# Real and imaginary halves of a scan swapped by ScalarE copies within PSUM instead of by a matmul

## The chip, the cores and the metric

One core of a Trainium2 chip runs the whole program. The metric is the device time of one execution in microseconds (us), as the median of several executions.

## The reference

A four-layer residual network on eight images of 64 channels and 128 x 128 points, all in float32. Layer 0 is a deformable convolution, layer 1 a 3 x 3 convolution, layer 2 a bidirectional state-space scan along rows and along columns, layer 3 a nearest-neighbour layer. The change is in layer 2, whose core is

```python
def _s5_scan(u, lam_re, lam_im, B_re, B_im, C_re, C_im, D, log_step):
    lam = lam_re + 1j * lam_im
    ...
    Bu = jnp.einsum('blh,ph->blp', u.astype(lam.dtype), B_bar)
    A = jnp.broadcast_to(lam_bar, Bu.shape)
    _, xf = jax.lax.associative_scan(_binop, (A, Bu), axis=1)
    _, xb = jax.lax.associative_scan(_binop, (A, Bu[:, ::-1]), axis=1)
    xs = jnp.concatenate([xf, xb[:, ::-1]], axis=-1)
    return 2.0 * jnp.real(jnp.einsum('blp,hp->blh', xs, Cc)) + D * u
```

with 64 complex states, on every image once with rows as the sequence and once with columns. Around it stand a layer norm before, a Gelu, a second layer norm and a product of small matrices after.

## The kernel before, in words

The eight images are handled as four pairs; a pair lies on 128 partitions (two images of 64 channels). First `deform` does layer 0 for all pairs: GpSimd (POOL) gathers, and VectorE (DVE) weights what was gathered. Then `rest` takes the four pairs one after the other, each through `conv3x3` (layer 1), `scan_layer` (layer 2) and, beside the next pair's work, `neighbours` (layer 3).

In the scan a complex state is kept as 128 partitions: its real part on the lower 64 and its imaginary part on the upper 64. A sequence is cut into groups of 4 x 256 points, 16 groups (`NG`) to a pair and direction. A complex rotation turns the recurrence into one with a real decay, which DVE's scan instruction can do; the rotation multiplies by a cosine, and adds the other half times a sine. For that second term the two halves must change places, one of them with its sign changed.

Three methods of `Scan` matter:

- `drive` makes the input of the recurrence: two matmuls into PSUM tile `pv`, a ScalarE (ACT) copy of it to SBUF tile `v` (L1256), a matmul of `v` with the constant 128 x 128 matrix `turn`, which swaps the halves and sets the sign, into PSUM tile `pt` (L1257), two DVE products of `pv` with cosines and of `pt` with sines (L1260), and their sum on POOL (L1261).
- `scan` runs the recurrence: a small matmul `pn` (L1269), an ACT copy of two columns (L1274), and two DVE scans into `z` (L1276).
- `rebuilt` turns a scan's result back: a matmul of it with `turn` into PSUM tile `zt` (L1301), a POOL product with cosines (L1305), a DVE product of `zt` with sines into `xt` (L1306), and their difference on POOL (L1307). For the backward scan the result comes back from device memory as `zb`.

`pv`, `pt` and `zt` share one PSUM pool tag, `b`, with two buffers; they take turns. `xt` and `v` have one buffer each.

Per pair these run in three stages, called A, B and C here:

- Stage A: `first_norm` (the layer norm, 8 steps) beside the backward scan along rows (`ways[0].back`). 16 drives.
- Stage B: `ways[0].ahead`, with `ways[1].back` beside it: per group one forward and one backward `drive`, two `rebuilt`, the output matmuls `py` (L1321), Gelu on ACT and a DVE sum `h` (L1323, L1324), the matmuls `pc` (L1339) with ACT's square and copy of them (L1340, L1342), the DVE chain `ln` of 15 small instructions that makes a reciprocal root (lines 112 to 122), a POOL product `ms` (L1353), transposes `tp` (L1357), and a DVE sum into the image, `room` (L1359).
- Stage C: `ways[1].ahead`, the same with one `drive` per group, plus DVE's `bn` statistics (L1362).

Each engine runs its own instructions strictly in the order that a scheduler writes down when the program is built. That order comes from the scheduler's own estimates, so a change to a few instructions can move all the others of the same stage. Where an instruction must wait for another engine, everything behind it on its own engine waits too.

Of the kernel before, what the change touches and what calls it, by code (L numbers as in the profile page):

```python
# [9 lines left out]
F32 = mybir.dt.float32  # L10
I32 = mybir.dt.int32
AF = mybir.ActivationFunctionType
ALU = mybir.AluOpType
# [3 lines left out]
P = 128  # L17
# [9 lines left out]
NS = 64  # L27
T = 4
NB = 256
# [13 lines left out]
class Net:  # L43
# [596 lines left out]
    def setup_scan(self, pp, ptag):  # L640
# [10 lines left out]
        tc, nc, ins, keep = self.tc, self.nc, self.ins, self.keep  # L651
        self.dirs = []
        with tc.tile_pool(name="b_scan_setup", bufs=1) as sp:
# [45 lines left out]
            sign = sp.tile([P, 1], F32, name="sign")  # L699
# [7 lines left out]
            swap = sp.tile([P, P], F32, name="swap")  # L707
            nc.vector.tensor_scalar(swap, col, swap_p, None, ALU.is_equal)

            self.turn = keep.tile([P, P], F32, name="turn")  # L710
            nc.vector.tensor_scalar(self.turn, swap, sign, -1.0, ALU.mult, ALU.mult)
            eye = self.ident

            qre, qim = (sp.tile([P, T + 1, 2], F32, name=f"q{n}") for n in ("re", "im"))
# [26 lines left out]
            for d in range(2):  # L741
# [8 lines left out]
                cs, sn = tabs[:, COS + 1 : COS + 1 + NB], tabs[:, SIN + 1 : SIN + 1 + NB]  # L750
# [15 lines left out]
                t2 = sp.tile([P, P], F32, tag="t2", name=f"t2_{d}")  # L766
                nc.vector.tensor_scalar(t2, swap, ssin[:, one], None, ALU.mult)
                nc.vector.scalar_tensor_tensor(tabs[:, ROT : ROT + P], eye, cs[:, NB - 1 : NB], t2, ALU.mult, ALU.add)

                u_, v_ = (sp.tile([P, 2, C], F32, tag=f"b{k}", name=f"b{k}_{d}") for k in "uv")  # L770
                for i in range(2):
# [444 lines left out]
class Scan:  # L1216
# [31 lines left out]
    def drive(self, f, g, fx):  # L1248

        nc, net, wp, tabs, tag = self.nc, self.net, self.wp, self.tabs, f"{self.p}_{self.d}{f}_{g}"  # L1250
        pv, pt = (net.ps.tile([P, 2, NB], F32, tag="b", name=f"{n}{tag}") for n in ("pv", "pt"))
        for h in range(2):
            at = MAT + (2 * f + h) * P
            nc.tensor.matmul(pv, lhsT=tabs[:, at : at + P], rhs=fx[:, :, h, :], start=h == 0, stop=h == 1)  # L1254
        v = wp.tile([P, 2, NB], F32, tag="v", name=f"v{tag}", bufs=1)
        nc.scalar.copy(v, pv)  # L1256
        nc.tensor.matmul(pt, lhsT=net.turn, rhs=v, start=True, stop=True)  # L1257
        u = wp.tile([P, 2, NB], F32, tag="u", name=f"u{tag}")
        for o, src, at in ((u, pv, COS), (v, pt, SIN)):
            nc.vector.tensor_mul(o, src[:, :, ::-1] if f else src, self.both(at + 1))  # L1260
        nc.gpsimd.tensor_add(u, u, v)  # L1261
        return u

    def scan(self, f, g, u, last, ztag):

        nc, wp, tabs, tag = self.nc, self.wp, self.tabs, f"{self.p}_{self.d}{f}_{g}"
        if last is not None:
            pn = self.net.ps1.tile([P, 2], F32, tag="bs", name=f"pn{tag}")
            nc.tensor.matmul(pn, lhsT=tabs[:, ROT : ROT + P], rhs=last[:, :, NB], start=True, stop=True)  # L1269
        z = wp.tile([P, 2, NB + 1], F32, tag=ztag, name=f"z{tag}", bufs=1 if ztag == "zbk" else 2)  # L1270
        if last is None:
            nc.vector.memset(z[:, :, 0:1], 0.0)
        else:
            nc.scalar.copy(z[:, :, 0], pn)  # L1274
        for i in range(2):
            nc.vector.tensor_tensor_scan(z[:, i, 1 : NB + 1], tabs[:, DEC : DEC + 1].to_broadcast([P, NB]), u[:, i, :], z[:, i, 0:1], ALU.mult, ALU.add)  # L1276
        return z
# [16 lines left out]
    def rebuilt(self, f, g, zf):  # L1294

        nc, net, wp, tag = self.nc, self.net, self.wp, f"{self.p}_{self.d}_{g}"
        if f:
            zf = wp.tile([P, 2, NB], F32, tag="zb", name=f"zb{tag}", bufs=1)
            nc.sync.dma_start(zf, net.back[self.d][g])
        pt = net.ps.tile([P, 2, NB], F32, tag="b", name=f"zt{f}{tag}")  # L1300
        nc.tensor.matmul(pt, lhsT=net.turn, rhs=zf[:, :, 0:NB], start=True, stop=True)  # L1301
        x = wp.tile([P, 2, NB], F32, tag=f"x{f}", name=f"x{f}{tag}", bufs=1)
        t = wp.tile([P, 2, NB], F32, tag="xt", name=f"xt{f}{tag}", bufs=1)
        o = x[:, :, ::-1] if f else x
        nc.gpsimd.tensor_mul(o, zf[:, :, 0:NB], self.both(COS))  # L1305
        nc.vector.tensor_mul(t, pt, self.both(SIN))  # L1306
        nc.gpsimd.tensor_sub(o, o, t)  # L1307
        return f, x
# [133 lines left out]
```

## Time and profile before

| | |
|---|---|
| median of 10 runs | 16339.99 us (16328.91 to 16344.98) |
| the profiled execution: time | 16343.99 us |
| the profiled execution: span of the core | 16342.2 us, mean granted clock 0.824 |
| busy: PE (matmul) | 10862.0 us, 66% |
| busy: DVE | 11670.0 us, 71% |
| busy: ACT | 2880.8 us, 18% |
| busy: POOL | 10189.8 us, 62% |
| `deform` | from the start to about 11740 us |
| pair 0: stages A, B, C | about 11914 to 12111, to 12431, to 12689 us |

Busy shares are means over stages with different limits. `deform` takes the first 72% and holds nothing of the scans' loops. In the scans one group of stage B follows the other after 21.4 us, one group of stage C after 15.7 us, and one step of stage A after 20.5 us.

### The profile page before, as it was taken

To read this page: it belongs to the slowest core of one execution; us is meant where nothing else is said; L and a number is where in the kernel's file an instruction comes from. 1 tells how busy PE (TensorE), PEld (TensorE's weight loads), DVE (VectorE), ACT (ScalarE), POOL (GpSimd) and SP (SyncE) were. 2 spreads that over 40 slices of the span, in tenths; PEclk is the share of its full clock that TensorE was granted. 3 is DMA by queue.
4 is the path that set the end of the run, shared out by engine and by line. 5 is a ranking of instruction groups with operands and counts; after the bars stand their busy time and mean duration, and the time that the engine had idled before them with its cause. 6 is when DMAs were issued, how large, how long until landed. Compare 5 with 4: busy or idle time off the path is not lost. (4 is left out here: it accounts for less than half of the span.)

```text
span 16342.2 us, 119261 instructions
## 1 busy us (share of the span) xinstructions
PE 10862.0 (66%) x31736; PEld 3994.6 (24%) x31736; DVE 11670.0 (71%) x27948; ACT 2880.8 (18%) x4762; POOL 10189.8 (62%) x10484
## 2 busy tenths in 40 slices
PE   7864676367665535766556655643489788888896
PEld 2211122112211111211111111111135344344343
DVE  6777777777777777777777777777547558466566
ACT  1100111011000001100000000000144254243342
POOL 5777777777777777777777777777425135044142
PEclk9986797678887767988778877865699899999997
DMA  5434444344433334443333333333422533434223
GB/s 172 126 120 134 138 144 151 111 140 149 147 114 118 115 112 139 147 124 115 118 115 115 115 119 115 114 108 108 125 65 68 151 80 101 119 82 135 88 68 107
DMA packets 900135, 1933.41 MB, mean 118 GB/s; under 512 B 199932, under 2 KB 435844, under 8 KB 876420
## 3 DMA queue, kind: packets, MB, share of 16 engines
q0 software_dynamic: 442368, 1208.55, 25.0%
q1 hardware_dynamic: 382048, 679.50, 13.6%
q10 hardware_dynamic: 75044, 37.72, 1.1%
q8 instruction: 257, 4.21, 0.1%
q14 instruction: 418, 3.42, 0.1%
HBM read 1540.74 MB, written 208.10 MB: 107 GB/s over the span
## 5 line engine op out<-in xcount | busy, mean ns | idle before, releaser
L380 POOL DMA_INDIRECT g<-table,idx x9216 | 8717.0, 946 | 2823.2 <-issue 2633.8
L391 DVE TENSOR_TENSOR g<-g,corner_weights 128x256 f32<-128x256 f32 x9216 | 3777.6, 416 | 2707.8 <-DMA g<-table,idx 2670.4
L392 DVE TENSOR_REDUCE sm<-g 128x64 f32<-128x256 f32 x9216 | 5018.3, 580 | 8.8
L292 PE MATMUL po<-xe,wt 128*54 128x512 f32 (+3 forms) x8384 | 4299.3, 628 | 13.1 <-ACT ob L302 13.0
L398 PE MATMUL sp<-ident,sm 128*128 128x128 f32 x4096 | 1536.1, 380 | 4156.8 <-DVE sm L392 4142.5
L398 PEld LDWEIGHTS sp<-ident,sm 128*128 128x128 f32 x4096 | 629.3, 155 | 6725.4 <-DVE sm L392 5020.5
L403 ACT COPY s<-sp 128x512 f32<-128x512 f32 x1024 | 599.8, 586 | 8717.5 <-PE sp L398 8717.1
L292 PEld LDWEIGHTS po<-xe,wt 128*54 128x54 f32 x8384 | 902.4, 132 | 1344.5 <-issue 1061.9
L409 PE MATMUL yp<-s,wd 128*64 128x512 f32 (+1 forms) x2560 | 898.2, 711 | 25.7 <-ACT s L403 24.8
L891 POOL COPY l_yb<-ln_y 128x512 f32<-128x512 f32 x128 | 72.8, 612 | 1300.6 <-DVE ln_y L122 1300.6
L1261 POOL TENSOR_TENSOR u<-u,v 128x512 f32<-128x512 f32 x256 | 327.9, 1281 | 688.1 <-DVE v L1260 553.4
L607 PE MATMUL c<-room,l_w 128*64 128x508 f32 (+1 forms) x3072 | 740.8, 597 | 23.3 <-DMA room<-nx 13.4
L1353 POOL TENSOR_TENSOR ms<-ms,ln_y 128x512 f32<-128x512 f32 x256 | 274.0, 1090 | 641.4 <-DVE ln_y L122 619.3
L1243 ACT ACTIVATE fx<-room,ln_b,ln_g 128x512 f32<-128x512 f32 x512 | 639.2, 1292 | 170.8 <-DMA in<-fx 149.5
L1276 DVE TENSOR_TENSOR_SCAN z<-tabs,z,u 128x256 f32<-128x256 f32 x512 | 435.4, 876 | 214.5 <-POOL u L1261 185.9
L1254 PE MATMUL pv<-in,tabs 128*128 128x512 f32 x1024 | 509.4, 620 | 43.6 <-DVE u L1260 40.7
L1339 PE MATMUL pc<-outs,h 128*128 128x256 f32 x2048 | 498.1, 386 | 29.1 <-DVE h L1324 26.8
L1321 PE MATMUL py<-x,outs 128*128 128x512 f32 x1024 | 504.3, 596 | 7.9 <-POOL x L1307 7.4
L1321 PE MATMUL py<-in,outs 128*128 128x512 f32 x1024 | 506.8, 608 | 2.9 <-ACT h L1323 2.3
L1339 PEld LDWEIGHTS pc<-outs,h 128*128 128x128 f32 x2048 | 393.2, 193 | 205.9 <-issue 113.3
L1307 POOL TENSOR_TENSOR x<-x,xt 128x512 f32<-128x512 f32 x256 | 347.9, 1359 | 131.8 <-DVE xt L1306 131.5
L609 DVE TENSOR_TENSOR room<-room,c 128x512 f32<-128x512 f32 x128 | 88.1, 688 | 438.6 <-PE c L607 435.4
(416 smaller groups left out, 10184.2 us busy)
## 6 DMA issues: line engine op xcount, KB each, us to landing
g<-table,idx POOLq DMA_INDIRECT x9216, 2.7
in<-fx SPq DMA_DIRECT2D x1024, 128.0 KB
xe<-in_x_dram SPq DMA_DIRECT2D x56, 1408.0 KB
table<-q SPq DMA_DIRECT2D x256, 256.0 KB
y<-ys SPq DMA_DIRECT2D x128, 256.0 KB
room<-in_x_dram SPq DMA_DIRECT2D x64, 512.0 KB
yr<-y SPq DMA_DIRECT2D x64, 512.0 KB
room<-nx SPq DMA_DIRECT2D x256, 128.0 KB
```

Source lines behind the costliest of these rows:

```text
L292: nc.tensor.matmul(po[:, r0:r1, c0:c1], lhsT=wt[:, t, :], rhs=xe[:, row + r0 : row + r1, c0 + dx : c1 + dx], start=n == 0, stop=n == len(u ...
L380: nc.gpsimd.indirect_dma_start(out=tq[:, k, :], out_offset=None, in_=flat[i], in_offset=bass.IndirectOffsetOnAxis(ap=idx[:, at : at + 1], ...
L391: nc.vector.tensor_mul(t[:, ks], t[:, ks], w)
L392: nc.vector.tensor_reduce(sm[:, ks], t[:, ks].rearrange("p k q c -> p k c q"), axis=mybir.AxisListType.X, op=ALU.add)
L398: nc.tensor.transpose(sp[:, j, :], sm[:, j * P : (j + 1) * P], self.ident)
L403: nc.scalar.copy(st[i][:, :, m * P : (m + 1) * P], sp)
L409: nc.tensor.matmul(yp[half[i], :], lhsT=wd[rows, j, :], rhs=src[rows, :], start=j == 0, stop=j == 4)
L607: nc.tensor.matmul(o, lhsT=lt, rhs=mv, start=k < 2, stop=k >= len(calls) - 2)
L1243: nc.scalar.activation(fx[:, e].rearrange("p h (o m) -> p h o m", m=self.INNER), src[:, e::2], AF.Identity, bias=w["ln1_b"], scale=w["ln1_g"])
L1254: nc.tensor.matmul(pv, lhsT=tabs[:, at : at + P], rhs=fx[:, :, h, :], start=h == 0, stop=h == 1)
L1321: nc.tensor.matmul(py, lhsT=lt, rhs=mv, start=n == 0, stop=n == len(calls) - 1)
L1339: nc.tensor.matmul(pc[:, i], lhsT=hs[:, h, i, m * P : (m + 1) * P], rhs=self.outs[:, CEN : MIX + P], start=True, stop=True)
```

## The change

In `drive` and in `rebuilt` the matmul with `turn` is gone. A new method `swap` writes the two halves of the PSUM tile by two ACT copies of 64 partitions each, the upper half of the source to the lower half of the target and the other way round. In `drive` they read `pv` in PSUM, and the copy of `pv` to SBUF is gone too; in `rebuilt` they read the scan's result in SBUF. The sign that was in `turn` is multiplied into the table of sines once, when the tables are made; `turn` is no longer made.

```diff
@@ setup_scan
-            self.turn = keep.tile([P, P], F32, name="turn")
-            nc.vector.tensor_scalar(self.turn, swap, sign, -1.0, ALU.mult, ALU.mult)
...
+                nc.vector.tensor_scalar(sn, sn, sign, None, ALU.mult)
@@ drive
+        self.swap(pt, pv)
         v = wp.tile([P, 2, NB], F32, tag="v", name=f"v{tag}", bufs=1)
-        nc.scalar.copy(v, pv)
-        nc.tensor.matmul(pt, lhsT=net.turn, rhs=v, start=True, stop=True)
         u = wp.tile([P, 2, NB], F32, tag="u", name=f"u{tag}")
         for o, src, at in ((u, pv, COS), (v, pt, SIN)):
             nc.vector.tensor_mul(o, src[:, :, ::-1] if f else src, self.both(at + 1))
         nc.gpsimd.tensor_add(u, u, v)
         return u
+
+    def swap(self, to, src):
+
+        for h in range(2):
+            self.nc.scalar.copy(to[h * NS : (h + 1) * NS], src[(1 - h) * NS : (2 - h) * NS])
@@ rebuilt
         pt = net.ps.tile([P, 2, NB], F32, tag="b", name=f"zt{f}{tag}")
-        nc.tensor.matmul(pt, lhsT=net.turn, rhs=zf[:, :, 0:NB], start=True, stop=True)
+        self.swap(pt, zf[:, :, 0:NB])
```

## The prediction

> **What bounds the kernel now.** I read first the page's forty slices, to see which stages the change can touch.
>
> ```profile
> PE   7864676367665535766556655643489788888896
> DVE  6777777777777777777777777777547558466566
> ACT  1100111011000001100000000000144254243342
> POOL 5777777777777777777777777777425135044142
> ```
>
> Up to slice 29 (about 11740 us) POOL and DVE work on the gathers of `deform`; from there on PE leads, and ACT has room. The turn matmuls are all in the last 4400 us. The costliest groups from 11800 us on give their price (busy us, mean ns, idle before):
>
> ```profile
> L1257 PE MATMUL pt<-v,turn 128*128 128x512 f32 x512 | 277.3, 623 | 80.0 <-ACT v L1256 77.4 <-ACT z L1274 1.8
> L1256 ACT COPY v<-pv 128x512 f32<-128x512 f32 x256 | 149.4, 584 | 543.4 <-POOL u L1261 323.5 <-PE pv L1254 216.6
> L1301 PE MATMUL zt<-z,turn 128*128 128x512 f32 x256 | 137.6, 620 | 12.8 <-DVE z L1276 12.8
> L1301 PE MATMUL zt<-zb,turn 128*128 128x512 f32 x256 | 132.7, 600 | 6.6 <-DVE u L1260 3.9 <-DMA zb<-back 2.7
> ```
>
> One matmul shows as two records. Then two stretches of pair 0, ten groups of stage B and ten of stage C (busy us of PE, PEld, DVE, ACT, POOL; clock; DMA):
>
> ```profile
> 12200.00:12414.40 214.40, 190.49 (x602) 101.81 (x601) 132.88 (x311) 99.58 (x180) 99.47 (x81) 1.00 0.29 74
> 12470.00:12627.20 157.20, 156.96 (x517) 88.82 (x517) 135.52 (x281) 68.65 (x140) 88.09 (x70) 1.00 0.21 51
> ```
>
> In C, PE has no gap at all: 15.70 of 15.72 us per group. DVE is next with 13.55. In B, PE is busy 19.0 of 21.4 us. The timeline of PE there names the two gaps:
>
> ```profile
> 12256.32 1.98 PE L1254 MATMUL pv<-in,tabs 128*128 128x512 f32 x4 [0.92 <-DVE u L1260]
> ...
> 12260.64 1.12 PE L1257 MATMUL pt<-v,turn 128*128 128x512 f32 x2 [1.48 <-ACT v L1256]
> ```
>
> By these views the change takes work from the engine that bounds. So the question is what comes next, and for that I need the in-order chain of DVE, POOL and ACT. Here it is in one group of C:
>
> ```profile
> 12565.17 2.06 POOL L1353 TENSOR_TENSOR ms<-ms,ln_y 128x512 f32<-128x512 f32 x2 [3.70 <-DVE ln_y L122]
> ...
> 12568.02 1.26 POOL L1261 TENSOR_TENSOR u<-u,v 128x512 f32<-128x512 f32 x1 [0.79 <-DVE v L1260]
> ...
> 12568.46 1.36 DVE L1324 TENSOR_TENSOR h<-h,in 128x512 f32<-128x512 f32 x1
> ...
> 12569.57 1.38 POOL L1305 TENSOR_TENSOR x<-zb,tabs 128x512 f32<-128x512 f32 x1 [0.29 <-POOL u L1261]
> ...
> 12569.75 2.40 DVE L1276 TENSOR_TENSOR_SCAN z<-tabs,z,u 128x256 f32<-128x256 f32 x2
> ```
>
> `h` takes 0.66 us at best, but 1.36 here, ending 0.54 after POOL's sum; two scans take 1.39 us elsewhere, but 2.40 here, ending 2.87 us after the sum. DVE operations with two SBUF inputs and POOL operations take turns.
>
> **The change, part by part.**
>
> *PE.* Four records in a row (12261.60, 1.88 us) start 0.43 us apart, so a turn costs PE 0.86 us. Removed per group: 4 turns in B (3.4 us), 3 in C (2.6 us), 2 per step of A (1.7 us). If PE stayed the bound, that would be the gain. The weights' loads lie beside other matmuls: nothing.
>
> *ACT.* Removed per drive: one copy of 0.584 us. Added per drive and per rebuild: two copies of 64 partitions. ACT's time goes with elements per partition (256 elements 0.37, 512 elements 0.58), so half the partitions save nothing. No row shows ACT writing PSUM: its bounds are 0.49 us (L1256 to the next ACT start, 12260.00 to 12260.49) and 0.69 (L923, a 512-element activation); I take 0.59. The built order gives the second copy a wait on the first, so the pair can't overlap: 2 x 0.59 + 0.05 = 1.23 us. ACT's load grows by 0.59 to 0.65 us per drive and 1.23 per rebuild: from 9.96 to about 13.7 us of 21.4 in B, from 6.87 to about 10 of 15.7 in C. ACT does not become the bound by load; what counts is what stands behind its waits.
>
> *The drive itself.* Before: copy 0.59 and turn 1.02 us; after: 1.23. 0.4 us shorter. The rebuild: turn 1.02 before, 1.23 after. 0.2 longer.
>
> *Order.* The built order differs in every scan group. In `deform` POOL's order, which sets the pace there, is the same to the last instruction: zero, with 15 us (0.1%) either way for DVE's and PE's few moved rows. The product of sines and sign, once per direction, and the dropped `turn` lie in that stage under the gathers: zero; without the cover under 1 us. SP issues the same DMAs; the four of an input land about 4.9 us after its second activation (SP's issue 2.38 us, then about 2), which in the walks below is in time.
>
> *Stage C, walked.* In the new order ACT runs: `h`(0), swap of `zb` (2), first half of the swap of `z`, `h`(1), its second half, then the squares. So `h`(1) stands behind a copy that waits for the DVE scans. DVE runs: u, v, h, scans, xt, h, xt, var, room, var, ln, room, ln, bn, ln, bn, 12 ln. Before, the second `room` and both `bn` came after the end of `ln`; now they stand ahead of it, and POOL's `ms`, with the sum of u and v queued behind it, waits for the last `ln`. Clock zero at that last `ln`: `ms` twice to 2.2; sum to 3.5; `h` to 4.0 and scans to 6.3 (as in the rows above); ACT's half swap to 6.95, `h`(1) to 7.45; DVE `h` waits for POOL's `x` (1.3 to 1.5 us from 6.5) and ends at 8.5; POOL's difference to 9.8; second `xt` (one buffer, so it waits for that) to 10.5; var 0.65, room 1.2, var 0.65, ln 0.2, room 1.2, two ln and two bn 1.6, 12 ln at 0.21 each 2.5: 18.4 us. PE's part (`pc` after `h`, transposes before room) ends inside this. With no turn-taking at all between DVE and POOL the same walk gives 16.6. I take 17.7, nearer the upper, because the same neighbours clash in the rows shown: +2.0 us per group over 15.7. Bounds +0.9 and +2.7.
>
> *Stage B, walked.* One chain runs through `h`, `pc`, the forward `pv` (now behind `pc`), the swap (ACT is then in the backward `fx`, two of 1.2 us, ahead of the second square), u, v, sum, scans, six `ln`, backward u and v, two swaps in a row on ACT, sum, scan, xt, difference, `py`. Clock zero at the first `py` from `x`: `pc` 4.4, `pv` done 8.4, swap done 10.5 (its halves stand on both sides of a square that waits for var), scans done 14.8, backward u 16.6, backward sum 18.6, second scan 20.9, difference 21.3, next `py` 21.35, the second difference 0.3 late: 21.7 us. With every turn between DVE and POOL lost: 24.0. In ten groups of C the means are 0.99 for `h` and 1.18 for a scan against 0.66 and 0.72, about half of a full clash; I take 22.7: +1.3 over 21.4, bounds +0.3 and +2.6. PE then idles about 7 us per group.
>
> *Stage A, walked.* After the last `l1v` matmul before, `fx` starts 6.3 us later (11991.64 to 11997.93) and the squares 11.2 later. In the new order a half swap that waits for the second `pv` stands ahead of `fx`, the other between two `fx`: the squares start at 12.3. The rest is the same 9.3 us: +1.1 per step, bounds +0.5 and +1.5.
>
> *Sum.* Per pair 8 x 1.1 + 14 x 1.3 + 14 x 2.0 = 55 us (14 of 16 groups are in steady order), four pairs +220 us. The profiled execution took 16343.99, 4 us over the median: 16344 + 220 - 4 = 16560 us. All lower bounds: 21 us per pair, 16424. All upper: 86 per pair, 16684.
>
> A rule on this: the Trainium skill, "SBUF — State Buffer", section "Who interferes with whom" has the port pair of DVE and GpSimd as an exclusive lock, held for the whole instruction. Taken alone that speaks for the full clash, and the sum would be near 16680; the means of C's rows show about half. Another, "ScalarE: Activation LUTs", section "What ACT_TABLE_LOAD costs", has 186 ns + 0.833 ns per element, 0.61 us for 512; the trace's copy from PSUM took 0.584. By an estimate from that page a pair costs 0.05 us more, under 10 us in all.
>
> **The rivals.**
>
> 1. *PE was the bound, and its time comes back.* For it: 100% PE in C, and scheduler orders that keep DVE under 14 us. C would fall to DVE's 13.55, B by 3.4 to 18.0: (2.2 + 3.4) x 14 x 4 = 310 us, 16030. Against it: the walked chains hold no PE wait that the removal shortens. It decides from the point where C's chain is below 15.7, 2 us shorter than I walked, and B's below 21.4. A half of it gives about 16190.
> 2. *The chains fall on the old periods*, within 0.6 us in sum: 16340.
> 3. *Copies are dearer*: 0.69 each and 0.21 of wait between halves (as ACT's gaps behind PE), 1.6 per pair. In B three pairs are on the chain (+1.1), in C one half (+0.2), in A +0.4: 86 us more, 16646.
>
> That the change does not do what it says is excluded by the built order: no turn matmul is left.
>
> **How the numbers follow.** The forecast (16424 to 16684) gets 0.65, rival 3 0.12, rival 2 0.06, rival 1 0.17. From 16300 to 16690 lie the forecast, most of rival 3, rival 2 and a weak form of rival 1: about 0.8. A measurement of this kernel can tell 0.2% (33 us) from no change. Faster: 0.17; within 0.2%: 0.06; slower: 0.65 + 0.12 = 0.77.
>
> **What would show it.** Right: in C, PE with gaps of 4 to 5 us per group, the period at 17 to 18, POOL's `ms` waiting for `ln_y` and ACT's `h` late behind the half swap; in B, PE under 75%; pairs of copies 1.2 us apart in start. Wrong: periods below 15.7 and 21.4, or copies under 0.5 us, or `deform` moved by over 20 us.

## The result, and the profile after

The changed kernel takes 16761.14 us (median of 8 runs, 16752.98 to 16767.23) against 16339.53 us (28 runs) for the kernel before: 1.0259 times as long, 95% interval 1.025 to 1.0268. The profiled span is 16757.0 us. The forecast was 16560 us with 16690 as the upper end: the direction was right, the size was about half.

The forty slices of the page after, with the row of the granted clock:

```profile
PE   7863676377666537766566556532877877777775
DVE  6777777777777777777777777777465665565665
ACT  1100110011000001100000000001353453453452
POOL 5777777777777777777777777776143142142241
PEclk9986898588787759888788778755888888888887
```

PE has fallen from 8 and 9 to 7 and 8 in the scans and ACT has risen by one or two, as planned. The row to look at is the last one: before, its slices 30 to 39 were `9899999997`; now they are `8888888887`. The last gather ends at 11661.8 us (11662.9 before), so nothing moved in `deform`. All of the loss lies behind it: 5095 us instead of 4679, +416.

To place it I take the spacing of the first Gelu of one group to that of the next, mean over eight groups in the middle of a stage. All four pairs agree within 0.1 us: B 21.44 before and 25.18 after, C 15.78 and 20.45. Stage A's steps are at 20.5 in both, but for pair 1 before, where most took 17.7 to 19.4. Two stretches of pair 0 after, ten groups of B and ten of C (columns as in the prediction: length; busy us of PE, PEld, DVE, ACT, POOL; clock; DMA):

```profile
12200.00:12450.40 250.40, 187.22 (x519) 94.65 (x518) 173.58 (x312) 132.17 (x239) 98.89 (x80) 0.87 0.25 62
12560.00:12764.50 204.50, 163.76 (x463) 96.11 (x462) 134.90 (x292) 95.16 (x191) 92.88 (x71) 0.83 0.19 49
```

Two things stand out against the rows of before. The granted clock was 1.00 in both and is 0.87 and 0.83; PE has fewer matmuls (463 records against 517 in C) and is busy longer (163.8 us against 157.0). And in B, DVE does the same instructions in 173.6 us that took 132.9.

**Stage C.** One group of its timeline after:

```profile
12643.31 2.38 DVE L1279 TENSOR_TENSOR_SCAN z<-tabs,z,u 128x256 f32<-128x256 f32 x2 [2.17 <-POOL u L1259]
...
12645.72 0.58 ACT L1265 COPY zt<-z 64x512 f32<-64x512 f32 x1 [4.54 <-DVE z L1279]
...
12646.24 0.59 ACT L1326 ACTIVATE h<-py 128x512 f32<-128x512 f32 x1
...
12648.06 3.78 PE L1342 MATMUL pc<-outs,h 128*128 128x256 f32 x8 [4.09 <-ACT ms L1345]
...
12652.30 1.19 DVE L1362 TENSOR_TENSOR room<-room,tp 128x512 f32<-128x512 f32 x1 [2.19 <-PE tp L1360]
```

Read it from the top. ACT's half swap waits 4.5 us for the scans, `h`(1) stands behind it, the first squares and copies of `pc` behind that; the second `pc` needs their PSUM buffer, so PE is idle for 4.09 us. Then come eight records of `pc` in 3.78 us. The same eight, ahead of the gap, took 1.89 (12641.86). So the transposes are late, and DVE's `room` waits 2.19 us for them. The granted clock in three stretches from there on (columns as above) names the reason:

```profile
12647.27:12654.10 6.83, 6.04 (x14) 4.12 (x15) 3.45 (x5) 4.09 (x12) 2.79 (x2) 0.50 0.35 79
12654.10:12667.75 13.65, 10.32 (x33) 5.47 (x31) 10.00 (x25) 5.44 (x9) 6.46 (x6) 1.00 0.06 19
12667.75:12674.58 6.83, 6.09 (x14) 4.12 (x15) 3.44 (x6) 4.09 (x12) 2.75 (x2) 0.50 0.34 77
```

Around the gap the clock is at half for 6.83 us, then full for 13.65. Both are whole multiples of 3.413 us, as are all distances between changes of the clock in this trace. Six such windows are 20.48 us, and C's spacings climb from 19.45 to 20.48 within the stage and stay there: the period seems to have locked to the clock's windows.

**Stage B.** DVE's costliest small instruction, first in ten groups of B after, then the same before (count, busy us, mean ns, idle before):

```profile
L121 DVE SCALAR_TENSOR_TENSOR ln_t<-ln_t,ln_ve 128x16 f32<-128x16 f32 x41 | 28.7, 701 | 1.1
```

```profile
L121 DVE SCALAR_TENSOR_TENSOR ln_t<-ln_t,ln_ve 128x16 f32<-128x16 f32 x40 | 7.0, 174 | 1.0
```

An instruction of 16 columns takes four times as long. The timeline of B shows why, and shows PE's gap too:

```profile
12369.20 1.26 POOL L1259 TENSOR_TENSOR u<-u,v 128x512 f32<-128x512 f32 x1 [1.94 <-DVE ln_t L120]
12369.23 1.25 DVE L121 SCALAR_TENSOR_TENSOR ln_t<-ln_t,ln_ve 128x16 f32<-128x16 f32 x1
...
12373.04 0.56 PE L1272 MATMUL pn<-z,tabs 128*128 128x2 f32 x2 [4.96 <-DVE z L1279]
12374.01 5.47 PE L1324 MATMUL py<-x,outs 128*128 128x512 f32 x8 [0.41 <-POOL x L1310]
```

The DVE instruction starts 0.03 us after POOL's and ends 0.02 us after it. In the new order POOL's sums, products and differences fall into the `ln` chain; four of its 15 instructions per group are held up in this way, and DVE is busy 4.1 us longer per group ((173.58 - 132.88) / 10). Behind the gap of 4.96 us, eight records of `py` take 5.47 us; in C at the full clock four take 1.88.

### The profile page after: what moved, and what is told of

Read it like the earlier page. It is cut to its first block, busy times and chain, and to the rows that moved or that the text cites. A ratio compares the mean times of both kernels' runs of the same rounds, so it can differ in the third digit from the quotient of the medians.

```text
span 16757.0 us, 118274 instructions
## 1 busy us (share of the span) xinstructions
PE 10764.8 (64%) x30712; PEld 3995.2 (24%) x30712; DVE 11884.6 (71%) x27949; ACT 3292.0 (20%) x5530; POOL 10218.6 (61%) x10484
## 5 line engine op out<-in xcount | busy, mean ns | idle before, releaser
L1342 PE MATMUL pc<-outs,h 128*128 128x256 f32 x2048 | 624.8, 451 | 274.6 <-ACT ms L1345 196.8
L607 PE MATMUL c<-room,l_w 128*64 128x508 f32 (+1 forms) x3072 | 736.0, 596 | 15.8 <-DMA room<-nx 9.6
L1324 PE MATMUL py<-x,outs 128*128 128x512 f32 x1024 | 608.6, 724 | 72.1 <-POOL x L1310 72.0
L1324 PE MATMUL py<-in,outs 128*128 128x512 f32 x1024 | 552.2, 647 | 9.0 <-DMA outs<-out_tab 9.0
L1342 PEld LDWEIGHTS pc<-outs,h 128*128 128x128 f32 x2048 | 433.9, 222 | 465.4 <-ACT ms L1345 247.1
L1362 DVE TENSOR_TENSOR room<-room,tp 128x512 f32<-128x512 f32 x256 | 294.9, 1152 | 146.2 <-PE tp L1360 145.1
```

What stands on the lines that cost most here:

```text
L607: nc.tensor.matmul(o, lhsT=lt, rhs=mv, start=k < 2, stop=k >= len(calls) - 2)
L1324: nc.tensor.matmul(py, lhsT=lt, rhs=mv, start=n == 0, stop=n == len(calls) - 1)
L1342: nc.tensor.matmul(pc[:, i], lhsT=hs[:, h, i, m * P : (m + 1) * P], rhs=self.outs[:, CEN : MIX + P], start=True, stop=True)
```

## The experiments

Theories: **order** (the loss is in the orders that the scheduler wrote for the copies: waits in line, PE's gaps, clashes of DVE and POOL), **copy** (a swap by two ACT copies costs what it costs, wherever it stands), and, as a part of the first, **clock** (PE runs at half rate behind its new gaps).

In drive_only, rebuilt_only and one_copy the scheduler wrote the order anew. For the others I hold stages to an order: for groups 4 to 14 of a stage, edges of issue order alone (no semaphore wait of their own) chain the instructions of an engine as a list says, in which `h1` is a group's second `h`, `pv0-` a `pv` emitted one group earlier:

```diff
+ORDER = {1: {"Activation": "z0 fx0 fx1 pt0- pt1- h0 zt0 zt1 h1 zt2 zt3 qs0 ms0 qs1 ms1 qs2 ms2 qs3 ms3", ...}}
...
+    def chain(self, marks):
+        for e, order in ORDER[self.d].items():
+            prev = None
+            for g in range(FIRST, LAST):
+                for w in order.split():
+                    i = by.get((g + w.count("+") - w.count("-"), e, w.strip("+-")))
...
+                    tc.add_manual_dep(i, prev.name, ... NoSync ...)
```

All results in one table: Gelu to Gelu spacing and granted clock in the middle of B and of C (pair 0, groups 5 to 13), the time behind the last gather, and the ratio to the kernel before with its interval. `drive_only`, `rebuilt_only`, `old_order`, `one_copy`, `all_tuned` and `matmul_b` ran on two other chips, on which the gathers last until about 14700 us and the kernel before takes 19383 and 19432 us; the stages behind the gathers can be compared (matmul_b's C, left as before, has 15.8 there too). A total that an expectation names is compared as 16340 us plus the difference behind the gathers. On those two chips the kernel before has no profile, and the medians give other differences: drive_only 165 us under the kernel before (81 behind the gathers), rebuilt_only 169 over (188), old_order 83 over (128), one_copy 330 over (381), all_tuned 78 under (40). So there the totals are good to about 85 us; the spacings don't depend on it.

| kernel | B us | C us | clock B, C | behind the gathers, us | ratio (95%) |
|---|---|---|---|---|---|
| before | 21.44 | 15.78 | 1.00, 1.00 | 4679 | 1 |
| changed | 25.18 | 20.45 | 0.87, 0.83 | 5095 | 1.0259 (1.025 to 1.0268) |
| drive_only | 18.61 | 16.58 | 1.00, 1.00 | 4598 | 0.9917 (0.9887 to 0.9947) |
| rebuilt_only | 20.09 | 20.56 | 1.00, 0.89 | 4867 | 1.0078 (1.0049 to 1.0106) |
| old_order | 21.97 | 16.87 | 0.91, 0.94 | 4808 | 1.004 (1.0024 to 1.0056) |
| one_copy | 24.71 | 20.48 | 0.93, 0.92 | 5060 | 1.0164 (1.0137 to 1.0191) |
| drive_c | 18.60 | 15.42 | 1.00, 1.00 | 4520 | 0.9911 (0.9894 to 0.9927) |
| squares_first | 20.73 | 15.52 | 0.97, 1.00 | 4688 | 1.0013 (1.0003 to 1.0023) |
| filler | 24.11 | 18.22 | 0.97, 1.00 | 4964 | 1.0183 (1.0166 to 1.02) |
| new_order | 24.89 | 17.79 | 0.92, 1.00 | 4937 | 1.0161 (1.0144 to 1.0178) |
| all_tuned | 19.16 | 15.52 | 0.99, 1.00 | 4639 | 0.9944 (0.9924 to 0.9964) |
| matmul_b | 19.18 | 15.76 | 1.00, 1.00 | 4604 | 0.9954 (0.9937 to 0.9972) |

In runs held to an order the last of these eight spacings is already of another kind. Groups 4 to 12 give, for B and C: old_order 22.46 and 17.14, squares_first 21.10 and 15.51, filler 23.88 and 18.00, new_order 24.99 and 17.67. Other pairs differ from pair 0 by up to 0.5 us (one_copy's B 24.21 to 24.72, squares_first's B 20.73 to 21.04).

**drive_only and rebuilt_only: one half of the copies each.** The other half stays a matmul with the swap matrix; the sign is in the sines in both.

```diff
+            self.turn = keep.tile([P, P], F32, name="turn")
+            nc.vector.tensor_copy(self.turn, swap)
# drive_only, in rebuilt:
-        self.swap(pt, zf[:, :, 0:NB])
+        nc.tensor.matmul(pt, lhsT=net.turn, rhs=zf[:, :, 0:NB], start=True, stop=True)
# rebuilt_only, in drive:
-        self.swap(pt, pv)
+        nc.scalar.copy(v, pv)
+        nc.tensor.matmul(pt, lhsT=net.turn, rhs=v, start=True, stop=True)
```

> Only `drive` swaps by ACT copies; `rebuilt` keeps a matmul with the unsigned swap matrix, and the sign is in the sines. As built, stage C has the order of the kernel before on every engine (pt only changes from PE to ACT); stage B has a new order. Order theory (the loss is in the orders that were built, with PE's gaps and its clock, not in the copies): C stays at 15.4 to 16.0 us per group with a granted clock of 1.00, and B lies between the old 21.4 and the new 25.0; in all 16340 to 16490 us. Copy theory (each pair of copies costs what it costs wherever it stands; half of the pairs are left): half of the loss in every stage, C near 18, 16550 us.

> Only `rebuilt` swaps by ACT copies; `drive` keeps its ACT copy and a matmul with the unsigned swap matrix. As built, stage C has one half pair of `zt` copies ahead of h(1) on ACT, and on DVE room and bn ahead of the end of ln, nearly as in the changed kernel. Order theory: C at 18 to 20.5 us and B at 22 to 25 us per group, 16550 to 16750 us. Copy theory: half of the loss, 16550 us, the same as with the other half of the pairs alone.

Equal numbers of copies, 64 pairs per image pair, and results on both sides of the kernel before: -81 and +188 us behind the gathers, or 16259 and 16528 us. The copy theory wanted the same for both. The order theory is right that the two differ and which one loses, but both came out below its ranges: drive_only is faster than the kernel before. Its B went below the old 21.4, to 18.6; its C rose to 16.6, since DVE's `h`(0) had moved behind the scans, where the expectation had C in the old order; and rebuilt_only's B is at 20.1, not 22 or more. Its C has the full loss of the changed kernel with two thirds of that stage's copies.

**one_copy: the price of a copy.**

```diff
-        for h in range(2):
-            self.nc.scalar.copy(to[h * NS : (h + 1) * NS], src[(1 - h) * NS : (2 - h) * NS])
+        self.nc.scalar.copy(to, src)
```

> As the changed kernel, but each swap is one ACT copy of 128 partitions instead of two of 64; the halves therefore keep their places (the exchange itself is left out). It takes away 0.6 us of ACT and one wait per swap, 128 swaps a pair. Order theory: the order as built in C is like that of the changed kernel, so most of the loss stays: 16600 to 16760 us. Copy theory: half of the loss goes, 16550 us or less.

C does not move (20.48), B by 0.5 us; 35 us of the 416 go, by the medians 92 of 422. Halving ACT's work on the swaps buys a twelfth to a fifth of the loss; +381 us behind the gathers are 16721 us, in the range of the order theory. C says less than it seems: it is again at six windows of the clock, with one of them at half rate (0.92) instead of two (0.83), so the lock can hide what a copy costs there.

**old_order and squares_first: all copies, in the order of the kernel before.** squares_first differs from old_order in ACT's order alone:

```diff
-ACT, C: z0 fx0 fx1 pt0- pt1- h0 zt0 zt1 h1 zt2 zt3 qs0 ms0 qs1 ms1 qs2 ms2 qs3 ms3
+ACT, C: z0 fx0 fx1 pt0- pt1- h0 zt0 zt1 h1 qs0 ms0 qs1 ms1 zt2 zt3 qs2 ms2 qs3 ms3
```

(in B the two `zt` copies of z and one `fx` move behind the first squares likewise, and the other `fx` moves ahead of the first `zt`).

> All swaps by ACT copies, as in the changed kernel, but ACT, DVE and PE run stages B and C of groups 4 to 14 in the order of the kernel before; the pairs of copies stand on ACT where their inputs are ready (drive's in the place of its old copy, rebuilt's ahead of each Gelu or behind the second one). Order theory: C at 15.0 to 16.5 us per group, B at 20 to 22, clock near 1.00, 16250 to 16420 us in all. Copy theory: ACT's longer load and the pairs' 1.2 us on the chain stay, so 16550 us or more.

> As old_order, but on ACT the pair of copies of z stands behind the first two squares and copies of pc, so that the second pc no longer waits for them behind a copy that waits for the scans. Order theory: the rest of old_order's loss was that place; C 15.0 to 16.0 us, B 19.5 to 21, granted clock 0.98 to 1.00, in all from the time of the kernel before to 1% under it. Copy theory: C stays at 16.9 and B at 22.

old_order takes away 3.2 us per group in B and 3.6 in C, with every copy still there; B is at or just over the upper edge of what I expected, C 0.4 to 0.6 us over it, and the total with 16468 us too. What was left shows in two groups of its C:

```profile
15708.36 3.47 PE L1358 MATMUL pc<-outs,h 128*128 128x256 f32 x8 [2.12 <-ACT ms L1361]
...
15726.09 1.99 PE L1358 MATMUL pc<-outs,h 128*128 128x256 f32 x8 [2.12 <-ACT ms L1361]
```

The second `pc` waits for ACT, whose copy of z stands ahead of the squares. Why equal gaps cost 3.47 us once and 1.99 the next time shows in the clock's windows around them, each pair of rows the window of the gap and the next one:

```profile
15705.31:15708.73 3.42, 1.30 (x7) 0.82 (x6) 2.49 (x5) 2.15 (x6) 2.06 (x3) 1.00 0.33 105
15708.73:15712.14 3.41, 3.41 (x11) 2.68 (x10) 1.27 (x2) 1.03 (x4) 1.98 (x2) 0.50 0.56 126
15722.38:15725.79 3.41, 1.59 (x8) 1.06 (x6) 3.04 (x4) 1.49 (x4) 2.05 (x2) 1.00 0.21 77
15725.79:15729.21 3.42, 3.12 (x16) 2.62 (x17) 2.05 (x4) 2.23 (x9) 2.62 (x3) 1.00 0.67 153
```

The first gap lies whole in one window, PE is busy for only 1.30 us of it, and the next window runs at half rate; the second gap reaches over an edge, PE is busy for 1.59 us, and the clock stays.

squares_first moves the copy of z behind the first squares. The wait is gone (the same `pc` then waits 1.00 us, for DVE's `h`), C is at 15.5 and B at 20.7 to 21.1, and the kernel is 0.13% over the one before, just outside the range that I gave. So 512 swaps on ACT, in place of the turns on PE, cost next to nothing when they stand in the right place. Its stretch in C also answers whether PE's load was the bound there:

```profile
12500.00:12600.00 100.00, 89.02 (x295) 48.73 (x293) 89.87 (x184) 62.26 (x122) 59.27 (x46) 1.00 0.19 48
```

PE is busy 89% of the time instead of 100%, and the period fell by 0.26 us. So less work on PE buys little there: of the 2.6 us per group that the turns took on PE, 0.26 come back.

**new_order: no swap by a copy, in the order of the changed kernel.** The kernel before with PE, ACT and DVE of B and C, and POOL of B, held to the changed kernel's lists; the turns stand on PE where the copies were, and ACT has only its copy of `pv`.

> The kernel before with its matmuls and its copy of pv, but groups 4 to 14 of stages B and C held to the order of the changed kernel on PE, ACT, DVE and POOL (turn matmuls placed where the copies stood; on ACT nothing stands between the two Gelus). Order theory: B 24 to 26 us with no swap by a copy at all; C 17 to 20 if DVE's order counts there, 15.7 to 16.5 if only the Gelu behind the half swap did. Copy theory: both stages at the old 21.4 and 15.8.

B comes to 24.89 us with matmuls alone: 3.45 of the 3.74 us that the change cost there. DVE is busy 17.4 us per group (139.1 in eight), as in the changed kernel. In C it is 17.79: the order of DVE and PE without any copy costs 2.0 us (which of the two, no run separates). Nothing stands between the Gelus on ACT here; PE's longest gap in a group is 0.95 us, and the clock is 1.00.

**filler: the clock.** The changed kernel in its own order, with matmuls that nobody reads in PE's two long gaps:

```diff
+            if FIRST <= g < LAST:
+                for _ in range(FILL[self.d]):
+                    self.nc.tensor.matmul(self.spare[:, P : P + NB], lhsT=self.tabs[:, ROT : ROT + P], rhs=self.tabs[:, COS + 1 : COS + 1 + NB], start=True, stop=True)
```

> The changed kernel in its own order, held to it for groups 4 to 14 of stages B and C, with extra matmuls of 128x256 that nobody reads in PE's two long gaps: 8 in B ahead of the second pn, 6 in C ahead of the second half of pc. Clock theory (the gap makes the granted clock fall, and the matmuls behind it run at half rate on the chain): clock 0.97 to 1.00, the second pc 1.9 us instead of 3.8, C 18.2 to 18.8 us, B 22.8 to 23.6, 150 to 250 us under the changed kernel, about 1.0% to 1.4% over the kernel before. Without it: C 20.4 and B 25.2 as in the changed kernel, or longer by some of the fill.

Lines of PE in one group of C (the second one is the fill):

```profile
12615.40 1.89 PE L1361 MATMUL pc<-outs,h 128*128 128x256 f32 x8
...
12617.34 2.75 PE L1400 MATMUL pn<-tabs 128*128 128x256 f32 x12
12621.58 1.99 PE L1361 MATMUL pc<-outs,h 128*128 128x256 f32 x8 [1.48 <-ACT ms L1364]
```

More work for PE, and the stage is faster: the second `pc` takes 1.99 us instead of 3.78, C falls from 20.45 to 18.22 and B from 25.18 to 24.11. Where the fill is in every group, C is at 18.00 and B at 23.7, just outside the range that I gave for B (22.8 to 23.6). In all 131 us come back, less than the 150 expected, and the ratio of 1.0183 is over the 1.0% to 1.4%; the first and last groups have no fill.

**drive_c, all_tuned, matmul_b: where the best time lies.** drive_c is drive_only with C held to the order of the kernel before (`h0` ahead of the scans again). all_tuned has all copies, with B in drive_only's order and C in squares_first's. matmul_b is the kernel before, with B alone in drive_only's order.

> As drive_only (copies in `drive`, matmul in `rebuilt`), but groups 4 to 14 of stage C are held to the order of the kernel before on PE, ACT and DVE; stages A and B are as in drive_only. Order theory: drive_only's 16.6 us in C came from DVE's h(0) standing behind the scans; with the old order C is at 15.8 or less. If PE's load was the bound of C before, it is 14.9 (15.78 less one turn of 0.86); if a chain was, 15.6 to 15.8. B stays at 18.6. In all 0.9 to 1.3% under the kernel before. Copy theory: C stays near 16.6.

> All swaps by ACT copies, stage B held to drive_only's order (the pairs of `zt` on ACT behind the last copy of pc, where ACT was idle 1.3 us), stage C to that of squares_first. Order theory: with the copies off the chain, B loses PE's last two turns (1.7 us) and comes to 17.0 to 18.4 us, C stays at 15.5; in all 1.0 to 1.5% under the kernel before. Copy theory (ACT's added 2.4 us per group count wherever they stand): B 19 to 21, in all no better than drive_c.

> The kernel before, matmuls and all, with stage B alone held to drive_only's order. It tells whether drive_only's gain in B came from the copies or from the order. If from the order: B 18.8 to 20.0 us with the matmuls too (PE's own load was 19.0 per group), in all 0.5 to 0.9% under the kernel before. If from PE's two turns that went: B 20.3 to 21.5, about the kernel before. C stays at 15.8 in both.

drive_c beats both kernels: 16220.59 us against 16369.05 for the kernel before in the same runs. Its C, 15.4 to 15.6 us in the four pairs, lies just under what I expected of a chain, and far from the 14.9 of a bound by PE. Half of the gain is order: matmul_b keeps every matmul, and B falls from 21.44 to 19.18 us. There PE is full:

```profile
15250.00:15400.00 150.00, 148.93 (x471) 78.88 (x470) 112.66 (x244) 77.64 (x143) 79.00 (x62) 1.00 0.32 79
```

Taking two turns off PE (drive_only, drive_c) then gives 0.6 us of the 1.7 that they cost, so here PE's load did hold B up, by that much. all_tuned missed (17.0 to 18.4 expected): taking off the other two as well gives 19.16, 0.6 more than drive_c, as its waits in seven groups of B tell (total us, times, longest):

```profile
PE pn L1289 <- ACT z L1294: 11.1, 7, 1.6
PE tp L1377 <- DVE room L1379: 10.7, 7, 1.5
```

On ACT the `zt` copies stand ahead of `fx`, and the two columns of `z` behind that, so PE waits for them. Better lists may exist; none was tried.

## Why the prediction was wrong in size

*Right.* Copies: a pair of `pt` takes 1.15 us, one of `zt` 1.20 (1.23 forecast), so rival 3 falls. `deform`: -1.1 us. The walk of C as far as it concerned DVE, ACT and POOL: from the last `ln` (12639.35) the scans end at 6.3 us (6.3 forecast), DVE's `h` at 8.3 (8.5), the second `xt` at 10.2 (10.5). ACT's `h` stands behind the half swap, and PE's gap is 4.1 us, as told.

*First step that failed: "PE's part (`pc` after `h`, transposes before room) ends inside this."* It was costed with the matmuls' durations of the profile before, all taken at a clock of 1.00. But the walk itself gave PE a gap of 4 to 5 us, and behind such a gap the clock is at half and `pc` takes 3.78 us instead of 1.89. `room` then starts 12.95 us after the last `ln` and the group ends at 20.45, not at 18.4. filler prices it: 2.2 us per group in C, 1.1 in B (2.5 and 1.5 where every group has the fill). The Trainium skill, "TensorE: Matmul & The Clock Gate", section "What's actually happening", states the rule that I left out: after an idle window of about 3.4 us the array's clock is at half rate, and matmuls that follow run so until it has been busy for about as long. Our rows agree on the factor of two (3.78 to 1.89) and on gaps of 4 us and more; old_order's two rows, 3.47 and 1.99 us behind equal gaps of 2.12 us, show that a shorter gap can do it too. The page has the window as free-running, and the changes of the clock at multiples of 3.413 us agree. An idle window was not needed, though: one in which PE was busy for 1.30 of 3.41 us was enough, and the measurement decides.

*Second: "I take 17.7, nearer the upper" and "I take 22.7".* Both were set between no clash of DVE and POOL and every clash, from the means of the order before. In the new order nearly every clash came: with the clock restored, filler's 18.0 to 18.2 in C and 23.7 to 24.1 in B stand beside the walks with all clashes, 18.4 and 24.0. The means of the old order said nothing about which neighbours the new one would make, and one was misread: a mean of 1.18 us for a scan is 2.37 for two, the full clash of the row shown (2.40), not half of it. The skill's page "SBUF — State Buffer", section "Who interferes with whom", gives the pair of ports to whoever comes first for the whole instruction, and B's rows (1.25 us for an instruction of 0.17, ended with POOL's) agree; the value that I said it spoke for, near 16680, was nearer than mine.

*Third, small: stage A.* +1.1 us per step was forecast; the steps stayed at 20.5, and `first_norm` went from 133 to 135 us per pair on average. The 20.5 us are again six windows of the clock, before and after, at a granted clock of about 0.86, so a longer chain need not show; that this is the reason is likely, and no run tests it.

Put together with these sizes, B costs 2.6 + 1.1 and C 2.7 + 2.2 us per group: 8.6 x 14 x 4 = 482 us. The periods say 3.74 + 4.67, 471 us; 416 were measured, since the first and last groups of a stage lose less.

*The rivals.* Rival 1 (PE was the bound) was right about a kernel that nobody had run: in B, in a better order, PE is the bound, and turns removed pay. In C there is little in it: with PE busy 89% instead of 100%, the period fell by 0.26 us. What sets the 15.5 us of C is open; DVE is busy for 90% of it.

The wider error is one of framing: I treated the order as a consequence to be walked and the copies as the change. All kernels here but one_copy compute the same result, and their times lie between 0.9911 and 1.0259 of the kernel before; moving a pair of copies behind two squares (old_order to squares_first) takes 1.4 to 1.6 us per group off C, more than the copies themselves cost.

## What to carry to other kernels

When instructions move to another engine and a scheduler writes the order, compare the orders engine by engine first: whatever the moved instruction waits for, all that stands behind it in line waits too. If a walk leaves PE idle for some microseconds, price the matmuls behind the gap at half rate (and look whether the period then falls on a whole number of the clock's windows, where it can hide other costs), and price each neighbour pair of DVE and POOL in the new order by itself, not by the old means. And an engine that is 100% busy is not shown to be the bound until less work on it has shortened the period: try the change with the old order held, and the old instructions in the new order, before judging it.

## What the runs showed of the hardware

- The granted clock of a single core's TensorE falls within one group: 3.78 us for eight records behind a gap of 4.09 us, 1.89 without one, and back at full rate about 6 us after work resumes (12648.06 to 12654.10). It changes only at edges 3.413 us apart. Behind a gap of 2.12 us the eight records took 3.47 us or 1.99, as the gap lay to the edges. Matmuls that nobody reads, put into the gap, made the kernel 0.8% faster.
- A loop can settle on the clock's windows: stage C of the changed kernel and of one_copy, and stage A of the changed kernel, run at 20.5 us, six windows, at granted clocks from 0.83 to 0.92. That the windows hold them there is inferred from this agreement.
- A one-input TENSOR_SCALAR of DVE (`ln_y`, L116, 16 columns) is held up by POOL like the ones with two inputs: 1.15 us in B after, 0.16 before. My sentence in the prediction, that it is operations with two SBUF inputs, was too narrow.
- ACT copies 64 partitions of 512 columns from one half of the partitions to the other into PSUM in 0.56 us from PSUM and 0.58 us from SBUF; the copy of 128 partitions from PSUM to SBUF before took 0.58.
